# A transformer block on one core: another order of the linear steps, residual rows in a key buffer, and a planner that counts the port of VectorE and GpSimd both ways

## The chip, the core and the metric

The kernel runs on one core of a Trainium2 chip. The metric is device time in microseconds (us), from the first to the last instruction of one launch; of the kernel before there are three timed runs, and one further execution was recorded by the hardware profiler. In the profile the engines are called PE (TensorE matmuls), PEld (its weight loads), DVE (VectorE), ACT (ScalarE), POOL (GpSimd) and SP (SyncE, which issues the DMAs). "L205" is line 205 of the kernel before.

## What is computed

A conditioned (adaLN) transformer block on x of 8 sequences of 1024 tokens by 512 features, all in float32, with 16 heads of 32 features and a hidden layer of 2048:

```python
mod = silu(condition) @ Wada + bada
sh_a, sc_a, gt_a, sh_m, sc_m, gt_m = jnp.split(mod, 6, axis=1)
xm = layernorm(x, g1, be1) * (1.0 + sc_a[:, None, :]) + sh_a[:, None, :]
x = x + gt_a[:, None, :] * attention(xm, Wqkv, Wproj, bproj)     # causal, 16 heads
xm = layernorm(x, g2, be2) * (1.0 + sc_m[:, None, :]) + sh_m[:, None, :]
h = gelu(xm @ W1 + b1, approximate=False)
x = x + gt_m[:, None, :] * (h @ W2 + b2)
```

## The kernel before, in words

**Blocks.** A sequence is cut into two halves of 512 tokens. A half is a block; there are 16, numbered 0 to 15, and an odd one attends to its own keys and to those of the even one ahead of it. So even blocks carry little attention and odd ones much, and the work repeats from pair to pair.

**Two streams.** One stream is attention. For each block and each group of four heads it makes score tiles (`scores`, L1602 on PE), of which DVE masks the diagonal (L1616) and takes the maxima (L1619); the maxima are split into three bfloat16 parts (L1638 to L1641, on POOL or DVE), turned into a row by PE (L1657) and copied by ACT (L1663). Then come the weights: PE subtracts the maxima (L1683) and forms the transposed scores (L1695), ACT takes the exponential (L1708), POOL clears the upper triangle (L1713), PE multiplies with v (L1736), and POOL adds the weights up for the denominator (L1821), which PE sums at a group's end (L1757). Score tiles and weight tiles share one PSUM tile of four banks, named st or sc: the next user of it waits until DVE or ACT is through with the last.

The other stream is linear work: the projections k, q, v (`k`, `q`, `v`), the attention output with the gate and the residual (`proj`), the norm and modulation (`norm_a` and `at` for attention, `mt` for the hidden layer, with PE transposes at L769), the hidden layer up (`u`, four steps) and down (`d`, four parts). Nearly all of its matmuls come from one helper, L205. They follow Strassen's scheme with 7 products in place of 8, each of 256 columns; a full step of 7 products is 448 rows of the trace. The sums of that scheme are elementwise work: from PSUM by DVE (L197) or ACT (L192), and from SBUF to SBUF by a helper `either` that takes DVE (L162) or POOL (L165). The down part has two such subtractions on the hidden tiles hT, of 128 by 1024 elements each, that always go to DVE (L1211), and two that `either` places. Three PSUM banks serve the linear stream, the transposes, L1657 and L1757.

**The planner.** The order of all instructions is written by the kernel's own Python code. It keeps a clock for PE, DVE, ACT and POOL (`now`) and the time at which each buffer is written and left (`written`, `left`). Attention goes in its fixed order; between two of its units, `step_aside` puts in linear matmuls until the next unit is due by these clocks. `plan[w]` lists the linear steps of window w, that is, beside the attention of block w. `note` books an instruction; with `port=True` it is a DVE instruction that has to let a POOL instruction under way finish first. `either` takes DVE where it would end more than `margin` ns ahead of POOL. `sooner` chooses between DVE and ACT.

**Order of a window.** Window w finishes the down parts of block w-2 or w-1, projects v of block w, makes the attention output of block w-1, k of w+1, `mt` of w-1, q of w+1, and then the up steps of w-1. The residual rows of a block (`load_xr`, four DMAs of 256 KB by SP) lie in the single buffer of pool `xrp`; only block 14 used a key buffer. Keys have three buffers in turn.

**DMA.** Weights come through a ring of nine tiles of 256 KB (`fetch`), issued by SP in the order in which they are used, one tile to each of the 7 products.

Of the kernel before, what the change touches and what calls it, by code (L numbers as in the profile page):

```python
# [22 lines left out]
def kernel(  # L23
# [80 lines left out]
    def due(reads=(), writes=()):  # L104
# [4 lines left out]
            t = max(t, left.get(k, 0.0))  # L109
        return t  # L110

    def note(engine, ns, reads=(), writes=(), port=False):
        start = max(now[engine], due(reads, writes))
        if port:
            start = max([start] + [b for a, b in pool_spans if a <= start < b])
        end = start + ns
        now[engine] = end
        if engine == "POOL":
            pool_spans.append((start, end))
            del pool_spans[:-16]  # L120
# [28 lines left out]
        t = due(reads, writes)  # L149
        return "DVE" if max(now["DVE"], t) + dve <= max(now["ACT"], t) + act else "ACT"  # L150

    margin = [1500]

    def either(out, a, b, op, reads, writes):

# [82 lines left out]
        0: [("load_xa", 2), ("preps",), ("k", 1), ("norm_a", 2), ("gates", "a"), ("q", 1)]  # L238
        + [("mod", 4), ("at", 2), ("v", 1), ("mod", 3), ("gates", "m")],
    }  # L240
    late = []
    for w in range(1, NB):
        n = w - 1
        m = mlp_steps(n)
        even = blocks[n][1] == 0
        rows_a = [("rows", blocks[n][0], "a")] if even else []
        rows_m = [("rows", blocks[n][0], "m")] if even else []
        own = m[:1] + ([("load_xa", w + 2)] if w + 2 < NB else []) + m[1:3]
        own += [("norm_a", w + 2)] if w + 2 < NB else []
        if w == NB - 1:  # L250
            steps = late[:1] + [("load_xr", n)] + rows_a + [("proj", n), ("mt", n)] + late[1:]
            steps += [("v", w)] + rows_m + own + m[3:6]
            late = m[6:]
        else:

            steps = late + [("v", w), ("load_xr", n)] + rows_a + [("proj", n), ("k", w + 1)]
            if w == 1:
                steps = [("load_xr", n)] + rows_a + [("k", w + 1), ("proj", n)]
            steps += [("mt", n), ("q", w + 1)] + rows_m + own
            at = [("at", w + 2)] if w + 2 < NB else []  # L260
            if blocks[w][1] == 0:

                late = m[3:4] + at + m[4:]
            else:
                steps += m[3:4] + at + m[4:6]
                late = m[6:]
        plan[w] = steps
    n = NB - 1
    plan[NB] = [("load_xr", n), late[0], ("beside", ("proj", n)), late[1], ("mt", n)] + mlp_steps(n)

    plain_proj = (NB - 2, NB - 1)
    kept_sums = {}
# [538 lines left out]
        return bank  # L811

    qTs, kTs, vs = {}, {}, {}
    projected, valued = set(), set()
    xm_of, hTs, hidden = {}, {}, set()

    SUMS = (("S1", "A21", "A22", ALU.add), ("S2", "S1", "A11", ALU.subtract),
# [78 lines left out]
    def strassen(step, x, dest, target, row, done, put=None, after={}):  # L896
# [91 lines left out]
        tail_key[0] = key  # L988
        start(tail())

    def project_T(step, store, pool, tag, done):

        n = step[1]
        dst = pool.tile([P, NC, TB], F32, tag=tag, name=f"{tag}_{n}")
# [335 lines left out]
    def perform(step):  # L1330
        kind = step[0]
        if kind == "mod":
            yield from modulation(step[1])
        elif kind == "columns":
            parameter_columns()
        elif kind == "turn":
            yield from turn_first()
        elif kind == "gates":
            yield from gates(step[1])
        elif kind == "load_xa":  # L1340
            x_pre[step[1]] = load_x(step[1])
            written["x", f"a{step[1]}"] = now["PE"] + 6000
        elif kind == "load_xr":
            n = step[1]
            b, h = blocks[n]
            if n == NB - 2:
                xr = kvp.tile([P, NTT, D], F32, tag="kT", name=f"xr_{n}")
            else:
                xr = xrp.tile([P, NTT, D], F32, tag="xr", name=f"xr_{n}")
            residual[n] = xr  # L1350
            for t in range(NTT):
                r0 = h * TB + t * P
                nc.sync.dma_start(xr[:, t, :], x[b, r0 : r0 + P, :])
                landed = max(now["PE"], stored.get(n, 0.0)) + LANDING + 700 * t
                written["xr", n, t] = landed
        elif kind == "norm_a":
            key = f"a{step[1]}"
            normalize(x_pre.pop(step[1]), key, [("x", key)] * NTT)
        elif kind == "at":
            n = step[1]  # L1360
            guards = [("m used", n - 3)] if n > 2 else [("v done", 0)] if n == 2 else []
            start(modulated(f"a{n}", *columns_of["a"], blocks[n][0], guards))
        elif kind == "beside":
            start(perform(step[1]))
        elif kind == "sums":
            sum_weights(step[1:])
        elif kind == "mt":
            n = step[1]
            guards = [("v done", n + 1)]
            start(modulated(f"m{n}", *columns_of["m"], blocks[n][0], guards))  # L1370
        elif kind == "k":
            yield [("free for k", step[1])], []
            yield from project_T(step, kTs, kvp, "kT", lambda: None)
# [450 lines left out]
    def attend():  # L1824
        previous = None
        for n in range(NB):
# [19 lines left out]
            stream["rate"] = planned_time(n) / mine * (0.7 if n == 0 else 1.0)  # L1846
            written["free for k", n + 2 if n % 2 else n + 1] = 0.0
            written["free for k", n + 1] = 0.0
            for g, k, n_slots, upto in slots:
                if (n, g) == groups[-1]:  # L1850
                    margin[0] = -2000
# [66 lines left out]
    needs = sum(exp_need(parts) for n in range(NB) for g in range(NC) for parts in weight_units(n, g))  # L1918
    needs += sum(score_need(*unit) for unit in units)
    for n in range(NB):  # L1920
        written["attended", n] = NEVER
# [81 lines left out]
```

## Time and profile before

| quantity | value |
|---|---|
| median of 3 runs | 3485.39 us (3484.59 to 3486.25) |
| the profiled execution, time | 3487.44 us |
| the profiled execution, span of the core | 3485.7 us |
| PE busy | 3448.3 us, 99% |
| DVE busy | 1905.0 us, 55% |
| ACT busy | 1286.7 us, 37% |
| POOL busy | 2074.5 us, 60% |
| HBM over the span | 132 GB/s |

How to read it: the profiled execution lies within 0.1% of the median. PE has work nearly all of the time, so that the waits that count are short and many; they are found in the list of what PE waited for, and in the timeline around single waits. A matmul's row in the timeline gives the start of a run of like matmuls and the time until the last has drained; because matmuls are pipelined, the time from the start of one run to the start of the next is the better measure of what the first one takes.

### The profile page before, as it was taken

The page shows a single profiled execution, that of the slowest core. Times are in us where ns is not written, and L with a number is a line of the kernel's source. Part 1 is how long each engine was busy: PE and PEld are TensorE (multiplying, and loading weights), DVE is VectorE, ACT ScalarE, POOL GpSimd, SP SyncE. Part 2 cuts the span into 40 slices and gives each one's busy share as a digit, 9 for nine tenths or more (in the row PEclk, how much of TensorE's full clock was granted, in tenths as well). Part 3 has the DMA queues.
Part 4 walks back from the last instruction along what each step waited for, and adds up shares of the span by engine and source line. Part 5 has one row for each costly group of instructions (what it writes and reads, how often), then busy time and mean ns, then how long its engine had stood idle before and what let it go on. Part 6 is the DMA issues. An engine that isn't in the chain of part 4 may idle for free.

```text
span 3485.7 us, 122756 instructions
## 1 busy us (share of the span) xinstructions
PE 3448.3 (99%) x55618; PEld 1776.1 (51%) x55618; DVE 1905.0 (55%) x2136; ACT 1286.7 (37%) x1420; POOL 2074.5 (60%) x2209
## 2 busy tenths in 40 slices
PE   8999999999999999999999999999999999999999
PEld 5544455445554554545545455454554545545445
DVE  6765664554645556465564655645546455554463
ACT  2335243352433524235152352514524244241531
POOL 3676755675466664576645766557664576644640
PEclk9999999999999999999999999999999999999999
DMA  6843334335353353633536335363443534435334
GB/s 213 271 144 86 117 110 150 120 105 172 107 167 102 105 174 104 186 95 100 173 98 186 98 111 159 101 186 98 129 140 101 183 101 135 130 100 153 90 121 136
DMA packets 350523, 466.84 MB, mean 134 GB/s; under 512 B 27460, under 2 KB 212092, under 8 KB 350004
## 3 DMA queue, kind: packets, MB, share of 16 engines
q1 hardware_dynamic: 349808, 458.73, 43.8%
q8 instruction: 438, 7.18, 0.9%
q14 instruction: 81, 0.66, 0.1%
q10 hardware_dynamic: 196, 0.28, 0.0%
HBM read 416.90 MB, written 41.99 MB: 132 GB/s over the span
## 4 chain that ended last, share of the span: by engine, by line
PE 94%; DVE 3%; POOL 1%; ACT 1%; issue 0%; DMA 0%; SPq 0%; DVEq 0%; ACTq 0%; POOLq 0%
PE bank L205 65%; PE sc L1602 9%; PE po L1736 8%; PE st L1695 7%; PE st L1683 3%; DVE mx L1619 2%; PE bank L1757 2%; PE bank L769 1%; PE bank L1657 1%; POOL pT L1821 0%; DVE sc L1616 0%; POOL mcols L1640 0%; DVE pT L1818 0%; POOL mcols L1641 0%; DMA ada<-in_L_cond_Wada_dram 0%
## 5 line engine op out<-in xcount | busy, mean ns | idle before, releaser
L1821 POOL TENSOR_TENSOR pT<-pT,pT 128x256 f32<-128x256 f32 (+3 forms) x1254 | 1174.5, 972 | 210.3 <-ACT pT L1708 119.2
L1708 ACT ACTIVATE pT<-st 128x2048 f32<-128x2048 f32 x288 | 541.1, 1879 | 1001.1 <-PE st L1695 908.8
L205 PE MATMUL bank<-w,hT 128*32 128x256 f32 x14336 | 795.5, 379 | 0.0
L1619 DVE TENSOR_REDUCE mx<-sc 128x4 f32<-128x2048 f32 (+3 forms) x384 | 665.6, 1754 | 140.3 <-PE sc L1602 133.7
L205 PEld LDWEIGHTS bank<-w,hT 128*32 128x32 f32 x14336 | 448.8, 110 | 335.6 <-issue 29.2
L205 PE MATMUL bank<-xm_m,w 128*32 128x256 f32 x8192 | 498.8, 380 | 0.0
L205 PE MATMUL bank<-t_m,w 128*32 128x256 f32 x6144 | 384.2, 380 | 0.1
L205 PEld LDWEIGHTS bank<-xm_m,w 128*32 128x32 f32 x8192 | 253.6, 110 | 238.8 <-issue 76.0
L1713 POOL TENSOR_SCALAR_AFFINE_SELECT pT<-pT 128x512 f32<-128x512 f32 x256 | 164.8, 661 | 308.8 <-ACT pT L1708 306.9
L1602 PE MATMUL sc<-kT,qT 32*128 32x512 f32 (+3 forms) x3072 | 329.1, 520 | 2.9 <-DVE mx L1619 1.9
L1616 DVE TENSOR_TENSOR sc<-sc,mask 128x1024 f32<-128x1024 f32 (+1 forms) x160 | 162.9, 1018 | 276.2 <-PE sc L1602 217.6
L1736 PE MATMUL po<-pT,v 128*32 128x512 f32 (+3 forms) x3072 | 306.0, 493 | 0.0
L1695 PE MATMUL st<-qT,kT 32*128 32x512 f32 (+3 forms) x3072 | 299.8, 486 | 0.0
L205 PEld LDWEIGHTS bank<-t_m,w 128*32 128x32 f32 x6144 | 193.0, 110 | 180.8 <-issue 54.2
L205 PE MATMUL bank<-xm_a,w 128*32 128x256 f32 x3968 | 248.8, 381 | 1.3 <-ACT xm_a L784 1.1
L197 DVE TENSOR_TENSOR hT<-bank,u_u 128x512 f32<-128x512 f32 x192 | 129.1, 686 | 151.2 <-PE bank L205 149.0
L165 POOL TENSOR_TENSOR qT<-top,rec 128x512 f32<-128x512 f32 x60 | 77.1, 1285 | 219.8 <-ACT rec L1775 219.8
L1602 PEld LDWEIGHTS sc<-kT,qT 32*128 32x128 f32 x3072 | 129.4, 183 | 150.9 <-ACT pT L1708 61.8
L205 PE MATMUL bank<-w,qT 128*32 128x256 f32 (+1 forms) x2944 | 191.4, 399 | 1.3 <-DVE qT L1782 1.3
L1153 ACT ACTIVATE hT<-hT,cols 128x512 f32<-128x512 f32 x256 | 164.2, 711 | 55.0 <-DVE hT L197 54.4
L205 PE MATMUL bank<-t_a,w 128*32 128x256 f32 x2944 | 183.3, 380 | 0.0
L165 POOL TENSOR_TENSOR hT<-hT,hT 128x1024 f32<-128x1024 f32 x28 | 79.7, 2868 | 167.6 <-DVE hT L1211 167.6
(232 smaller groups left out, 3507.5 us busy)
## 6 DMA issues: line engine op xcount, KB each, us to landing
w<-in_L_cond_W_dram SPq DMA_DIRECT2D x384, 256.0 KB, 2.9
w<-kept_up_S SPq DMA_DIRECT2D x256, 256.0 KB, 2.6
w<-kept_down_S SPq DMA_DIRECT2D x256, 256.0 KB, 2.8
w<-kept_qkv_S SPq DMA_DIRECT2D x180, 256.0 KB, 2.7
w<-in_L_cond_Wqkv_dram SPq DMA_DIRECT2D x147, 256.0 KB, 3.0
hat<-in_x_dram SPq DMA_DIRECT2D x64, 256.0 KB, 4.7
xr<-in_x_dram SPq DMA_DIRECT2D x64, 256.0 KB, 4.6
out_dram<-xr SPq DMA_DIRECT2D x64, 256.0 KB, 2.6
```

What stands on the lines that cost most here:

```text
L165: nc.gpsimd.tensor_tensor(out, a, b, op)
L197: nc.vector.tensor_tensor(out, src, other, op)
L205: nc.tensor.matmul(ps[r, :], lhsT[:, r], rhs, start=start, stop=stop, skip_group_check=True)
L1153: nc.scalar.activation(hT[:, i, :], hT[:, i, :], AF.Gelu, bias=cols[:, O_B1 + f : O_B1 + f + 1])
L1602: nc.tensor.matmul(sc[:, j, c0 : c0 + w], qTs[n][r, gg, ts(qt, P)], keys_of(n, kh)[r, gg, :w], start=True, stop=True, skip_group_check=True,)
L1616: nc.vector.tensor_tensor(place, place, shape_of.to_broadcast(place.shape), ALU.add)
L1619: nc.vector.tensor_reduce(maxima[n, gg][:, kh, qt, :], sc[:, :, c0 : c0 + w], axis=AX.X, op=ALU.max)
L1695: nc.tensor.matmul(st[:, j, c0 : c0 + w], kT[r, gg, ts(k % NTT, P)], qT[r, gg, TB - w :], start=False, stop=True, skip_group_check=True,)
L1708: nc.scalar.activation(pT[:, :, :used], st[:, :, :used], AF.Exp, scale=scale)
L1713: nc.gpsimd.affine_select(diagonal, diagonal, pattern=[[0, HPG], [1, P]], compare_op=ALU.is_ge, fill=0.0, base=0, channel_multiplier=-1,)
L1736: nc.tensor.matmul(po[r, TB - w :], v[:, k % NTT, g * P + j * hd : g * P + (j + 1) * hd], pT[:, j, c0 : c0 + w], start=(k == 0), stop=last ...
L1821: nc.gpsimd.tensor_tensor(into, into, pT[:, j, c0 : c0 + w], ALU.add)
```

## The change

Four things are edited.

1. **The order of a window.** From window 3 on: the last up steps of block w-2 (they are now cut in two after the second step where block w is even), rows, residual load, v of w, the output of w-1, `mt` of w-1, then the four down parts of block w-2, then q and k of w+1, then the up steps of w-1. So the down parts are taken one window later than the hidden layer that they belong to, beside the norm of the next block.
2. **Residual rows.** Since a block's output is now made ahead of the down parts of the block before it, two blocks' residual rows are held at once: those of odd blocks go to an even key buffer that is free at that time, those of even blocks to the one buffer in `xrp`. The load waits in the plan for a new entry, "free for xr". Key buffers get fixed names. The first scores of a block wait in the plan for q and for k.
3. **The planner's port.** `note` now also holds a POOL instruction back while a DVE instruction that is booked with `port=True` runs (to 250 ns ahead of its end), and `give_way` moves POOL instructions that were already booked behind such a DVE instruction that starts before them.
4. `margin` goes from 1500 to 1000.

```diff
     shape = [None]
-    pool_spans = []
+    pool_spans, port_spans = [], []
+    FREE = 250
...
+    def give_way(start, end):
+
+        if not any(start <= a < end for a, *_ in pool_spans):
+            return
+        for i, (a, b, reads, writes) in enumerate(pool_spans):
+            if a < start:
+                continue
+            if a >= end:
+                break
+            later = end, end + b - a
+            pool_spans[i] = *later, reads, writes
+            for of, keys in ((left, reads), (written, writes)):
+                for k in keys:
+                    if of.get(k) == b + SYNC:
+                        of[k] = later[1] + SYNC
+            end = later[1]
+        now["POOL"] = max(now["POOL"], end)
+
     def note(engine, ns, reads=(), writes=(), port=False):
         start = max(now[engine], due(reads, writes))
         if port:
-            start = max([start] + [b for a, b in pool_spans if a <= start < b])
+            start = max([start] + [b for a, b, *_ in pool_spans if a <= start < b])
+            give_way(start, start + ns - FREE)
+        elif engine == "POOL":
+            start = max([start] + [b for a, b in port_spans if a <= start < b])
         end = start + ns
         now[engine] = end
-        if engine == "POOL":
-            pool_spans.append((start, end))
+        if port:
+            port_spans.append((start, end - FREE))
+            del port_spans[:-16]
+        elif engine == "POOL":
+            pool_spans.append((start, end, reads, writes))
             del pool_spans[:-16]
...
-    margin = [1500]
+    margin = [1000]
...
-    late = []
+    late, downs = [], []
     for w in range(1, NB):
...
-        own = m[:1] + ([("load_xa", w + 2)] if w + 2 < NB else []) + m[1:3]
-        own += [("norm_a", w + 2)] if w + 2 < NB else []
+        at = [("at", w + 2)] if w + 2 < NB else []
+        ups = m[:1] + ([("load_xa", w + 2)] if w + 2 < NB else []) + m[1:3]
+        ups += ([("norm_a", w + 2)] if w + 2 < NB else []) + m[3:4] + at
+        head = rows_a + [("load_xr", n)]
+        if w == 1:
+            steps = head + [("k", w + 1), ("proj", n), ("mt", n), ("q", w + 1)]
+        elif w == 2:
+            steps = downs[2:] + [("v", w)] + head + [("proj", n), ("mt", n), ("q", w + 1), ("k", w + 1)]
+        elif w < NB - 1:
+            steps = late + head + [("v", w), ("proj", n), ("mt", n)] + downs + [("q", w + 1), ("k", w + 1)]
+        else:
+            steps = late + head + [("v", w), ("proj", n), ("mt", n)] + downs
+        cut = m[2] if blocks[w][1] == 0 else None
+        i = ups.index(cut) if cut in ups else len(ups)
+        plan[w] = steps + rows_m + ups[:i]
+        late, downs = ups[i:], m[4:]
+        if w == 1:
+            plan[w] += downs[:2]
         if w == NB - 1:
...
-        else:
-
-            steps = late + [("v", w), ("load_xr", n)] + rows_a + [("proj", n), ("k", w + 1)]
...
-            steps += [("mt", n), ("q", w + 1)] + rows_m + own
...
+            plan[w] += late + downs[:2]
+            downs = downs[2:]
...
+    def key_tag(n):
+        return "odd_kT" if n % 2 else f"even_kT_{n // 2 % 2}"
...
-            if n == NB - 2:
-                xr = kvp.tile([P, NTT, D], F32, tag="kT", name=f"xr_{n}")
+            if n % 2:
+                yield [("free for xr", n)], []
+                spare = key_tag(min(n + 3, NB))
+                xr = kvp.tile([P, NTT, D], F32, tag=spare, name=f"xr_{n}", bufs=1)
             else:
                 xr = xrp.tile([P, NTT, D], F32, tag="xr", name=f"xr_{n}")
...
-                landed = max(now["PE"], stored.get(n, 0.0)) + LANDING + 700 * t
+                landed = max(now["PE"], stored.get(n - 1, 0.0)) + LANDING + 700 * t
...
-        until(lambda: units[unit_at[0]][0] in projected)
+        until(lambda: units[unit_at[0]][0] in projected & keyed)
```

The instructions themselves are the same in kind and number on PE; which of DVE, ACT and POOL takes an elementwise step is decided anew by the planner.

More of the change, by code (lines that the diff above doesn't have):

```diff
@@ L247 @@
         rows_m = [("rows", blocks[n][0], "m")] if even else []
-        own = m[:1] + ([("load_xa", w + 2)] if w + 2 < NB else []) + m[1:3]
-        own += [("norm_a", w + 2)] if w + 2 < NB else []
-        if w == NB - 1:
-            steps = late[:1] + [("load_xr", n)] + rows_a + [("proj", n), ("mt", n)] + late[1:]
-            steps += [("v", w)] + rows_m + own + m[3:6]
-            late = m[6:]
-        else:
-            steps = late + [("v", w), ("load_xr", n)] + rows_a + [("proj", n), ("k", w + 1)]
-            if w == 1:
-                steps = [("load_xr", n)] + rows_a + [("k", w + 1), ("proj", n)]
-            steps += [("mt", n), ("q", w + 1)] + rows_m + own
[L260 to L267, printed above, removed]
+        at = [("at", w + 2)] if w + 2 < NB else []
[16 more added lines that the diff above has]
+            plan[w] += downs[:2]
+        if w == NB - 1:
+            plan[w] += late + downs[:2]
+            downs = downs[2:]
     n = NB - 1
-    plan[NB] = [("load_xr", n), late[0], ("beside", ("proj", n)), late[1], ("mt", n)] + mlp_steps(n)
+    plan[NB] = [("load_xr", n), downs[0], ("beside", ("proj", n)), downs[1], ("mt", n)] + mlp_steps(n)
     plain_proj = (NB - 2, NB - 1)
@@ L813 @@
     qTs, kTs, vs = {}, {}, {}
-    projected, valued = set(), set()
+    projected, keyed, valued = set(), set(), set()
     xm_of, hTs, hidden = {}, {}, set()
@@ L1372, in perform @@
             yield [("free for k", step[1])], []
-            yield from project_T(step, kTs, kvp, "kT", lambda: None)
+            yield from project_T(step, kTs, kvp, "kT", lambda: keyed.add(step[1]))
         elif kind == "q":
@@ L1848, in attend @@
             written["free for k", n + 1] = 0.0
+            written["free for xr", n - 1] = 0.0
             for g, k, n_slots, upto in slots:
@@ L1920 @@
     for n in range(NB):
+        written["free for xr", n] = 0.0 if n == NB - 1 else NEVER
         written["attended", n] = NEVER
```

5 lines of the change are left out of this document (4 added, 1 removed).

## Prediction, made before the changed kernel ran

> **What bounds the kernel now.** I read the page first, then busy time by stretches, then what PE waited for, then the timeline around each kind of wait.
>
> ```profile
> PE 3448.3 (99%) x55618; PEld 1776.1 (51%) x55618; DVE 1905.0 (55%) x2136; ACT 1286.7 (37%) x1420; POOL 2074.5 (60%) x2209
> ...
> 989.00:1417.10 428.10, 426.74 (x6951) 219.43 (x6954) 230.02 (x258) 162.15 (x179) 263.45 (x279) 1.00 0.45 132
> ```
>
> PE is busy 99%. The second row is one pair of blocks, with the busy time of PE, PEld, DVE, ACT and POOL, at full granted clock (1.00): 428.10 us, PE busy for 426.74. The order of instructions shows as many PE instructions of each kind in the changed kernel. So its matmul time stays, and two things can change: what PE waits for, and what it pays where one form of matmul follows another. The waits, in the list for 420 to 3045 us (first three rows) and that for 80 to 420 us (last two):
>
> ```profile
> PE bank L1657 <- POOL mcols L1641: 4.4, 6, 0.7
> PE bank L769 <- ACT xm_m L784: 1.8, 6, 0.3
> PE sc L1602 <- DVE mx L1619: 1.4, 6, 0.5
> ...
> PE st L1683 <- DVE mx L1619: 2.4, 3, 1.5
> PE bank L1657 <- POOL mcols L1641: 1.3, 2, 0.6
> ```
>
> Six occurrences are one for each pair: a planned order that meets the same wait again and again. The list counts only idle time; what a wait costs is the lateness of a start against undisturbed matmuls, whose pace a long piece of the chain gives:
>
> ```profile
> 561.27 58.27 PE bank L205 x1080
> ```
>
> That is 54.0 ns for a row of 256 columns, 107.9 for one of 512.
>
> **The change, part by part.**
>
> *Waits of PE for the maxima rows (L1657).* In POOL's, DVE's and PE's timelines at the first of the six:
>
> ```profile
> 557.88 0.25 POOL L1638 CAST mcols<-mx 128x16 bf16<-128x16 f32 x1 [0.90 <-DVE mx L1633]
> 558.50 1.16 POOL L1640 CAST mcols<-rest 128x16 bf16<-128x16 f32 x1
> 559.74 1.07 POOL L1641 TENSOR_TENSOR mcols<-rest,mcols 128x16 bf16<-128x16 f32 x1
> 558.33 2.35 DVE L1211 TENSOR_TENSOR hT<-hT 128x1024 f32<-128x1024 f32 x2
> 559.05 1.07 PE L205 MATMUL bank<-w,hT 128*32 128x256 f32 x16
> 560.86 0.41 PE L1657 MATMUL bank<-ident_b,mcols 128*32 128x128 bf16 x16 [0.74 <-POOL mcols L1641]
> ```
>
> A split step of 0.25 us takes 1.16 and 1.07 while DVE's two subtractions run, and each ends as one of these ends: the two engines keep each other out. PE's 16 rows end at 559.05 + 16 x 0.054 = 559.91; L1657 starts at 560.86, 0.95 us late (0.92 without the few hundredths of a normal change). In the changed order the split of the odd block's second group is followed on DVE by steps that read PSUM (L197, v), not by L1211, and 9.4 us of PE work stand between the last scores and L1657 in place of 6.4. In even blocks the first two splits mostly go to DVE; no cover in the pairs is shorter than the shortest one of before (5.5 us), which caused no wait. Gain 6 x 0.92 = 5.5 us; bounds 0 and 5.5.
>
> *Waits between score tiles.* PE and DVE rows at one of them, with an undisturbed neighbour behind, and PE rows at the other kind:
>
> ```profile
> 1330.39 2.29 DVE L1619 TENSOR_REDUCE mx<-sc 128x4 f32<-128x2048 f32 x1
> 1330.62 1.93 PE L205 MATMUL bank<-xm_m,w 128*32 128x256 f32 x32
> 1332.73 0.71 PE L1602 MATMUL sc<-kT,qT 32*128 32x512 f32 x4 [0.18 <-DVE mx L1619]
> 1340.76 1.05 PE L205 MATMUL bank<-xm_m,w 128*32 128x256 f32 x16
> 1341.73 1.14 PE L1602 MATMUL sc<-kT,qT 32*128 32x512 f32 x8
> 1342.80 1.93 PE L205 MATMUL bank<-t_m,w 128*32 128x256 f32 x32
> ...
> 1370.32 0.64 PE L205 MATMUL bank<-xm_m,w 128*32 128x256 f32 x8
> 1370.78 1.91 PE L205 MATMUL bank<-t_m,w 128*32 128x256 f32 x32
> 1372.80 0.71 PE L1602 MATMUL sc<-kT,qT 32*128 32x512 f32 x4
> ```
>
> At 1340.76, 16 rows (0.86) and a change of form bring the scores at 1341.73: linear to scores costs 0.11. Scores to linear: 1342.80 - 1341.73 - 8 x 0.108 = 0.21. At 1330.62, 32 rows and the change end at 1332.46, the scores start 0.27 late; at 1370.32, 40 rows end at 1372.59, 0.21 late. In the second case the cover from the end of the scores is 0.21 + 40 x 0.054 + 0.11, about 2.5 us, against a reduction of 2.29 us and its latency of some 0.4. In the order, 14 scores have this short cover before the next; one has it in the changed kernel, the others at least 2.9 us. Gain 7 x 0.48 = 3.4. By the same count four other score tiles of the changed order come about 0.3 short: loss 1.1. Net gain 2.2; bounds 0 and 3.4.
>
> *Waits of the transposes.* PE rows and ACT's:
>
> ```profile
> 673.52 0.40 PE L205 MATMUL bank<-t_a,w 128*32 128x256 f32 x4
> 673.85 0.66 PE L769 MATMUL bank<-ident,xh_m 128*128 128x128 f32 x4
> 674.44 0.64 PE L205 MATMUL bank<-t_a,w 128*32 128x256 f32 x8
> 674.54 0.78 ACT L784 ACTIVATE xm_m<-bank,shiftm,gainm 128x512 f32<-128x512 f32 x1 [1.46 <-PE bank L769]
> 675.38 0.33 PE L769 MATMUL bank<-ident,xh_m 128*128 128x128 f32 x1 [0.30 <-ACT xm_m L784]
> ```
>
> Into a transposed bank that ACT empties until 675.32, PE comes back after 8 rows: it could start at 674.44 + 0.43 + 0.12 = 674.99 (0.12 from the first two rows) and is 0.39 late. Beside q and k, Strassen's scheme holds two banks; in the changed order `mt` runs beside the down parts, which hold one, and the transposes go in pairs into the other two. Gain 6 x 0.39 = 2.3; bounds 0 and 2.3.
>
> *The first pair (80 to 420 us).*
>
> ```profile
> 350.02 6.08 POOL L165 TENSOR_TENSOR hT<-hT,hT 128x1024 f32<-128x1024 f32 x2 [3.99 <-DVE hT L1211]
> 353.80 2.85 DVE L162 TENSOR_TENSOR qT<-top,rec 128x512 f32<-128x512 f32 x1
> 360.23 0.39 PE L1683 MATMUL st<-mrow,minus_ones 32*128 32x512 bf16 x4 [1.45 <-DVE mx L1619]
> ```
>
> A DVE product of 512 elements takes 2.85 us beside POOL's two long subtractions, so the maxima behind it are late and PE waits 1.45. In the changed kernel these subtractions are DVE's. That and the waits for L1657 there (1.3) may go: 2.8. But in block 0 one score tile of the fourth group gets 1.8 us of cover in place of a sufficient one, against a mask (0.70, by its row below), a reduction and latency of 0.7 + 2.3 + 0.4 = 3.4: loss 1.5. Net gain 1.3; bounds -3 and 4.
>
> *Changes of form.* Before there are 1101 between the forms of scores and of linear work and 131 from or to transposes; after, 1133 and 97. The first split into 17 more at 0.21 and 15 more at 0.11: 5.2 us. The second, 34 fewer at 0.12: -4.1. Loss 1.1; bounds 0 and 3.
>
> *Work that moves between engines.* The groups by line:
>
> ```profile
> L165 POOL TENSOR_TENSOR hT<-hT,hT 128x1024 f32<-128x1024 f32 x28 | 79.7, 2868 | 167.6 <-DVE hT L1211 167.6
> L165 POOL TENSOR_TENSOR hT<-hT 128x1024 f32<-128x1024 f32 x19 | 57.5, 3038 | 0.0
> L162 DVE TENSOR_TENSOR hT<-hT 128x1024 f32<-128x1024 f32 x13 | 19.4, 1508 | 0.0
> L1211 DVE TENSOR_TENSOR hT<-hT,hT 128x1024 f32<-128x1024 f32 x32 | 37.6, 1216 | 0.0
> L1821 POOL TENSOR_TENSOR pT<-pT,pT 128x512 f32<-128x512 f32 x504 | 633.2, 1290 | 121.8 <-ACT pT L1708 119.2
> L1713 POOL TENSOR_SCALAR_AFFINE_SELECT pT<-pT 128x512 f32<-128x512 f32 x256 | 164.8, 661 | 308.8 <-ACT pT L1708 306.9
> L1616 DVE TENSOR_TENSOR sc<-sc,mask 128x512 f32<-128x512 f32 x64 | 44.7, 699 | 134.4 <-PE sc L1602 107.3 <-issue 27.1
> L1616 DVE TENSOR_TENSOR sc<-sc,mask 128x1024 f32<-128x1024 f32 x96 | 118.2, 1231 | 141.8 <-PE sc L1602 110.3 <-ACT top L1770 12.2 <-ACT xh_m L653 11.5
> L1619 DVE TENSOR_REDUCE mx<-sc 128x4 f32<-128x1536 f32 x64 | 112.5, 1757 | 2.2
> ```
>
> POOL loses 28 + 18 of these: some 135 us of its 2074.5. DVE gains 46 at 1.22 to 1.51 us, 56 to 69 us on 1905.0. Both keep room, but DVE works in order, and it is tight at one place in each odd block: in the third group (six blocks, 3 to 13) a score tile's mask (1.23) and reductions (1.76 and a third of that) stand behind v3 (L197, as a mask of 512), two L1211 and two moved subtractions: 1.23 + 2.4 + 0.7 + 4 x 1.22 = 9.2 us of DVE work, with 8.6 of PE's from one tile's scores to the next. Counted on, DVE ends about 0.3 us ahead of PE's next weights if nothing holds it; with one hold by POOL's triangle step (0.66) it is 0.4 late. I take 0.2 x 6 = 1.2; what a worse case costs is a rival below.
>
> At this place a rule of the Trainium skill speaks against the change (SBUF — State Buffer, "SBUF: two separate sides"): a VectorE step with two inputs in SBUF and a GpSimd step that reads SBUF exclude each other for a whole instruction, and the one that starts first wins. The stretched 0.25 us steps and the 2.85 us product agree with it. By it, each moved subtraction also shuts out POOL's sums; that would change the result only where a sum is waited for.
>
> *At no cost.* The residual loads are 4 DMAs a block as before. SP stands at them until the last weights of a block have read the key buffer, with weight loads queued behind; nine tiles of 64 rows at 0.054 are 31 us of PE work, and that cover is longer than the tail of a block. Without it, each late tile would stop PE for its landing. The extra wait for k costs nothing while linear work is left to put in. I take 0 for the stretch after 3045 us, where the last steps are unchanged; bounds -3 and 3.
>
> **The sum.** 5.5 + 2.2 + 2.3 + 1.3 - 1.1 - 1.2 = 9.0 us off the profiled 3487.44 (span 3485.7), or 3478.4. The median lies 2.05 below that execution: 3485.39 - 9.0 = 3476.4.
>
> **The rivals.**
> - *The gain is given back in small new waits.* For: all scores are planned to within some 0.1 us of DVE's end, and DVE gets 56 to 69 us more. Against: fewer scores fall short by count. If half of the 10.0 us of the pairs returns, 3481.4.
> - *DVE is held by POOL's sums at the tight place; slower.* If the four subtractions there each let one sum of 1.29 us go first, DVE is 5.2 - 0.3 = 4.9 late, in six blocks 29 us: 3485.39 - 10.2 + 29 = 3504; with three holds, 3497. It decides from 17 us on, 2.9 us a block. For: POOL's sums are 633 us. Against: L1211's mean of 1.22 us over 32 shows them seldom held, and by the order POOL has just ended one set of sums there.
> - *All new tightness proves harmless.* All bounds on the good side, 5.5 + 3.4 + 2.3 + 4: 15.2 off, and 3 at the end: 3467.
> - *The planner changes nothing that PE feels,* the waits only move: 3485.
>
> **How the numbers follow.** The forecast has 0.50, the good side 0.12, the small new waits 0.19, no effect 0.06, the port 0.13. A measurement tells 0.2% (7 us) from no change: faster is below 3478.4, slower above 3492.4. The forecast, uncertain by some 4 us, lies below 3478.4 in nearly nine of ten: 0.45 with 0.12 is 0.57 faster; 0.05 + 0.19 + 0.06 is 0.30 the same; 0.13 slower. The range for 8 in 10 is 3466 to 3490; the forecast's own is 3470 to 3483.
>
> **What would show it.** Right: a pair of blocks near 426.5 us; no waits for L1641 and few for L1619 from 420 us on; POOL's hT groups nearly gone; L1640 and L1641 near 0.25 to 0.35. Wrong: a wait of L1683 for L1619 in every odd block, with L162 hT far over 1.22 us; waits for weight DMAs; or PE rows with more idle time after 3045 us.

## The result, and the profile after

| quantity | before | after |
|---|---|---|
| median | 3484.75 us (3483.65 to 3486.25, 9 runs) | 3496.5 us (3491.06 to 3500.8, 9 runs) |
| ratio to before, 95% interval | | 1.0032 (1.0022 to 1.0042) |
| the profiled execution | 3487.44 us | 3495.71 us |

The changed kernel is slower by 0.32%, where 0.2% can be told from no change; the forecast was 3476.4 us, and the time lies above the whole range. Its runs also differ by 10 us among themselves, those of before by under 3.

The head of the page after, and then busy time from 420 to 3045 us in the kernel before (first of the two rows) and after (second), columns as in the prediction:

```profile
span 3494.0 us, 122624 instructions
...
PE 3450.0 (99%) x55618; PEld 1792.7 (51%) x55618; DVE 2022.6 (58%) x2234; ACT 1289.5 (37%) x1438; POOL 1963.2 (56%) x2083
```

```profile
420.00:3045.00 2625.00, 2616.49 (x42600) 1346.80 (x42592) 1417.64 (x1590) 991.34 (x1090) 1621.29 (x1733) 1.00 0.44 131
```

```profile
420.00:3045.00 2625.00, 2604.52 (x42332) 1356.46 (x42324) 1522.56 (x1673) 990.90 (x1105) 1524.97 (x1610) 1.00 0.44 130
```

The loss is in the pairs of blocks: in the same 2625 us PE is idle 12.0 us longer (2616.49 - 2604.52). What it waits for there, in the list of waits of PE after, from 420 to 3045 us:

```profile
PE bank L230 <- ACT rec L1801: 11.1, 9, 2.7
PE bank L230 <- ACT xm_m L810: 2.4, 6, 0.4
PE sc L1636 <- ACT pT L1742: 1.8, 1, 1.8
PE bank L1691 <- POOL mcols L1675: 1.6, 1, 1.6
PE bank L795 <- ACT xm_m L810: 1.0, 1, 1.0
PE st L1717 <- DVE mx L1653: 0.8, 5, 0.2
...
PE sc L1636 <- DVE mx L1653: 0.6, 2, 0.3
```

Lines moved by some 25 to 35: L205 is L230 now, L1619 L1653, L1641 L1675, L1657 L1691, L1683 L1717, L1708 L1742, L784 L810. The six waits for POOL's split (4.4 us) are gone, and one of 1.6 us is new. Nearly all else that is new has ACT behind the arrow, that is, as its releaser: an engine that is busy 37% and whose new order the prediction did not cost. L1801 is the logarithm of a group's denominators: PE sums them into one of the three linear banks (L1791), and ACT's logarithm frees that bank.

**The place in odd blocks.** PE's, ACT's and SP's rows in the timeline after, in block 7 (start, duration, engine, line):

```profile
1435.50 0.38 SPq L751 DMA_DIRECT2D xm_a<-turned_a  x1
...
1439.94 1.04 PE L1791 MATMUL bank<-pT,ones 128*32 128x512 f32 x8
...
1441.98 0.64 PE L230 MATMUL bank<-w,qT 128*32 128x256 f32 x8
1442.60 2.22 ACT L810 ACTIVATE xm_a<-xm_a,shifta,gaina 128x512 f32<-128x512 f32 x3 [3.60 <-DMA w<-kept_down_S]
...
1444.73 0.57 ACT L1801 ACTIVATE rec<-bank 128x512 f32<-128x512 f32 x1
...
1445.36 4.49 PE L230 MATMUL bank<-w,hT 128*32 128x256 f32 x48 [2.73 <-ACT rec L1801]
```

PE's sums are in their bank by 1441, but ACT does its work in order, and ahead of the logarithm stands the modulation of the next block's rows (L810, input xm_a). Those rows are turned by way of DRAM: four writes (L745) and one load (L751). The load, issued at 1435.50, lets ACT go on at 1442.60; the name behind the arrow is another transfer that landed then, but L810 reads only the turned rows. ACT stands 3.60 us, takes 2.22 for the modulation, and then frees the bank. PE is idle for 2.73. The same in the list of ACT's waits from 420 to 3045 us, first before, then after:

```profile
ACT xm_a L784 <- DMA xm_a<-turned_a: 128.9, 10, 16.8
```

```profile
ACT xm_a L810 <- DMA xm_a<-turned_a: 14.4, 7, 5.9
```

The list puts some of these waits under other names, the 3.60 us of block 7 among them. Counted by the steps themselves, ACT stood at these rows for 157.8 us in twelve places before, and for 22.8 in eleven after. In the kernel before nothing of PE was behind it: copies of v came next, and ACT stood another 14.8 to 23.1 us at each of those. The new order makes v earlier, and the logarithm takes the place behind the rows.

**The clock.** Busy time after, in three stretches that follow on this wait (the granted clock is the third number from the end of a row):

```profile
1442.00:1445.40 3.40, 0.67 (x16) 0.18 (x15) 1.78 (x3) 2.80 (x5) 0.00 (x0) 1.00 0.42 114
1446.20:1449.60 3.40, 3.40 (x40) 1.78 (x36) 3.40 (x5) 0.11 (x1) 2.44 (x2) 0.55 0.09 8
1449.70:1453.00 3.30, 3.30 (x60) 1.71 (x52) 3.30 (x3) 0.00 (x0) 3.17 (x2) 1.00 0.35 84
```

After the idle time the clock is halved for about 3.4 us: 40 rows in place of 60. That is another 1.7 us, which no list of waits shows, since PE counts as busy. It comes a second time behind a wait of 2.20 us near 2735 us, and nowhere between 420 and 3045 us in the kernel before. How long ACT stands differs from pair to pair, and with it both prices; that this also makes the spread of 10 us is argued here, and tested below.

**The place in even blocks.** PE's and ACT's rows after, in block 8:

```profile
1615.93 1.04 PE L1791 MATMUL bank<-pT,ones 128*32 128x512 f32 x8
1616.31 1.28 ACT L1185 ACT_TABLE_LOAD   x1
...
1617.60 2.56 ACT L1185 ACTIVATE hT<-hT,cols 128x512 f32<-128x512 f32 x4
1617.98 3.23 PE L230 MATMUL bank<-xm_m,w 128*32 128x256 f32 x56
...
1620.18 1.28 ACT L170 ACT_TABLE_LOAD   x1
1621.47 0.60 ACT L1801 ACTIVATE rec<-bank 128x512 f32<-128x512 f32 x1
...
1622.12 1.94 PE L230 MATMUL bank<-t_m,w 128*32 128x256 f32 x32 [0.91 <-ACT rec L1801]
```

Here four GELUs, with a table load on each side, stand ahead of the logarithm: 5.1 us. PE's 56 rows end at 1617.98 + 56 x 0.054 = 1621.00, so the next start is 1.12 late; five such places make 5.6 us.

### The profile page after: what moved, and what is told of

Read it like the earlier page. It is cut to its first block, busy times and chain, and to the rows that moved or that the text cites. A ratio compares the mean times of both kernels' runs of the same rounds, so it can differ in the third digit from the quotient of the medians.

```text
span 3494.0 us, 122624 instructions
## 1 busy us (share of the span) xinstructions
PE 3450.0 (99%) x55618; PEld 1792.7 (51%) x55618; DVE 2022.6 (58%) x2234; ACT 1289.5 (37%) x1438; POOL 1963.2 (56%) x2083
## 4 chain that ended last, share of the span: by engine, by line
PE 93%; ACT 2%; DVE 2%; DMA 2%; issue 0%; SPq 0%; POOL 0%; ACTq 0%; DVEq 0%; POOLq 0%
PE bank L230 65%; PE sc L1636 8%; PE po L1770 7%; PE st L1729 7%; PE st L1717 3%; PE bank L1791 1%; DVE mx L1653 1%; PE bank L795 1%; DMA xm_a<-turned_a 1%; ACT pT L1742 1%; DMA turned_a<-xm_a 1%; PE bank L1691 0%; ACT xm_a L810 0%; ACT hT L1185 0%; DVE sc L1650 0%
## 5 line engine op out<-in xcount | busy, mean ns | idle before, releaser
L1855 POOL TENSOR_TENSOR pT<-pT,pT 128x256 f32<-128x256 f32 (+3 forms) x1254 | 1230.4, 1016 | 194.7 <-ACT pT L1742 123.5
L1742 ACT ACTIVATE pT<-st 128x2048 f32<-128x2048 f32 x288 | 540.9, 1878 | 1025.5 <-PE st L1729 907.9
L230 PE MATMUL bank<-w,hT 128*32 128x256 f32 x14336 | 821.5, 381 | 9.0 <-ACT rec L1801 6.6
L1653 DVE TENSOR_REDUCE mx<-sc 128x4 f32<-128x2048 f32 (+3 forms) x384 | 665.7, 1754 | 210.9 <-PE sc L1636 204.7
L230 PEld LDWEIGHTS bank<-w,hT 128*32 128x32 f32 x14336 | 454.4, 110 | 374.0 <-issue 82.0
L230 PE MATMUL bank<-xm_m,w 128*32 128x256 f32 x8192 | 499.9, 380 | 0.1
L1747 POOL TENSOR_SCALAR_AFFINE_SELECT pT<-pT 128x512 f32<-128x512 f32 x256 | 177.8, 712 | 445.2 <-ACT pT L1742 443.5
L230 PE MATMUL bank<-t_m,w 128*32 128x256 f32 x6144 | 384.2, 380 | 4.7 <-ACT rec L1801 4.6
L230 PEld LDWEIGHTS bank<-xm_m,w 128*32 128x32 f32 x8192 | 256.0, 110 | 223.1 <-issue 60.9
L230 PEld LDWEIGHTS bank<-t_m,w 128*32 128x32 f32 x6144 | 190.7, 110 | 181.7 <-issue 54.5
L230 PE MATMUL bank<-xm_a,w 128*32 128x256 f32 x3968 | 239.8, 381 | 2.0 <-ACT xm_a L810 1.1
L230 PE MATMUL bank<-w,qT 128*32 128x256 f32 (+1 forms) x2944 | 192.9, 399 | 0.0
L230 PE MATMUL bank<-t_a,w 128*32 128x256 f32 x2944 | 181.2, 380 | 0.0
L230 PEld LDWEIGHTS bank<-xm_a,w 128*32 128x32 f32 x3968 | 127.4, 110 | 95.6 <-issue 12.6
```

Of the source, the lines that this page charges most:

```text
L230: nc.tensor.matmul(ps[r, :], lhsT[:, r], rhs, start=start, stop=stop, skip_group_check=True)
L1653: nc.vector.tensor_reduce(maxima[n, gg][:, kh, qt, :], sc[:, :, c0 : c0 + w], axis=AX.X, op=ALU.max)
L1742: nc.scalar.activation(pT[:, :, :used], st[:, :, :used], AF.Exp, scale=scale)
L1747: nc.gpsimd.affine_select(diagonal, diagonal, pattern=[[0, HPG], [1, P]], compare_op=ALU.is_ge, fill=0.0, base=0, channel_multiplier=-1,)
L1855: nc.gpsimd.tensor_tensor(into, into, pT[:, j, c0 : c0 + w], ALU.add)
```

## The experiments

The theory that was tested: ACT's queue, with the turned rows and the GELUs ahead of the logarithm, costs what the change was to gain and more. The main rival: DVE's added load and the port that it shares with POOL. All times are medians; the kernel before ran beside each, at 3484.1 to 3485.4 us.

**e1_order_alone.** The changed kernel with `note` and `margin` of before.

```diff
-            give_way(start, start + ns - FREE)
-        elif engine == "POOL":
-            start = max([start] + [b for a, b in port_spans if a <= start < b])
...
-    margin = [1000]
+    margin = [1500]
```

> The new order of work with the residual rows in a key buffer, but the planner's accounting of before (DVE waits for POOL only, margin 1500). Theory, ACT's queue: the waits of PE that the changed kernel has come from the order of the work (the turned rows' modulation, L810, stands ahead of the logarithm, L1801, which frees the bank of the product with d; four GELUs stand ahead of it in even blocks), so they stay: 3492 to 3500 us, at least 10 of the 13 waits of a bank for L1801 still there. Rival, the port: the cost comes from the accounting that moves hT subtractions to DVE; without it the time is at or below the kernel before's, 3477 to 3486 us, with POOL's busy time back near 2070 us.

3509.88 us, ratio 1.0068 (1.0056 to 1.0081): 13.4 above the changed kernel. Its waits of PE from 420 us on (lines are 25 lower there: L1666 is L1691, L1692 L1717, L1717 L1742, L1776 L1801):

```profile
PE bank L1666 <- ACT pT L1717: 8.3, 4, 2.1
PE st L1692 <- DVE mx L1628: 6.2, 10, 1.1
PE bank L205 <- ACT rec L1776: 6.0, 8, 0.9
```

Neither theory gave so much. The logarithm is waited for in 8 places, not 10, and waits at the maxima come on top. The name in the first row misleads: at one of its places the exponential (L1717) and POOL's last split step both end at 1498.81, and what L1666 reads is the split:

```profile
1498.54 0.27 POOL L1650 TENSOR_TENSOR mcols<-rest,mcols 128x16 bf16<-128x16 f32 x1
...
1498.85 0.23 PEld L1666 LDWEIGHTS <-mcols 128*32 128x32 bf16 x16 [2.26 <-POOL mcols L1650]
```

This is a wait for POOL's split, of the kind that the change was to remove, here 2.1 us long and in five places (four in the first row). So the new accounting does not cause the loss: within the new order it saves 13 us. By the rival the time should have fallen.

**e2_port_alone.** The plan and buffers of before, with the new accounting and margin.

```diff
+            give_way(start, start + ns - FREE)
+        elif engine == "POOL":
+            start = max([start] + [b for a, b in port_spans if a <= start < b])
...
-    margin = [1500]
+    margin = [1000]
```

> The order and the buffers of before with the new accounting alone (ports both ways, margin 1000). Theory, ACT's queue: copies of v stand behind the turned rows as before and nothing of PE waits for them; DVE's load rises by some 50 us without harm: 3479 to 3486 us, with the six waits of the maxima rows for POOL's split (0.92 us each) fewer or gone, and no stretch of halved clock after 420 us. Rival, the port: DVE is late at the score tiles and the time is that of the changed kernel or above, 3493 to 3500 us.

3519.02 us, ratio 1.0096 (1.0081 to 1.0112): 34 us above the kernel before. One row of its waits carries most of it (L1708 is L1683 of before, L1644 L1619):

```profile
PE st L1708 <- DVE mx L1644: 20.9, 24, 1.1
```

DVE's maxima are late four times in a pair. The theory's number was wrong, and for this order the rival holds. But the same accounting that costs 34 us here saves 13 in the new order, so it has no price of its own.

**e9_margin_alone.** The kernel before with the margin alone.

```diff
-    margin = [1500]
+    margin = [1000]
```

> The kernel before with one number of the accounting changed, the margin at 1000 ns in place of 1500. Theory: few hidden sums change engine, so the time stays within 3 us of the kernel before, 3482 to 3489 us, and the 34 us that the new accounting alone cost (e2_port_alone) come from DVE and POOL counted as holding each other, which moves scores in the order. Rival: the order of before is so finely set that any change of the planner's counts costs tens of us: 3500 us or more.

3502.58 us, ratio 1.005 (1.0036 to 1.0064): half of those 34 us from one number. The rival's time is right, and the theory's first step was wrong: many hidden sums change engine. Of the 64 that `either` places, POOL had 47 before and has 13 here, as many as in e2_port_alone. So half of that kernel's loss comes with these moves, and the other half with the counting of the port. Whether DVE's load or the shifted order is what costs is not shown. Its waits are small and come six times each, once a pair; two of its rows:

```profile
PE sc L1602 <- ACT pT L1708: 4.6, 6, 0.8
PE bank L1657 <- POOL mcols L1641: 4.5, 6, 0.7
```

**e3_rows_later.** The changed kernel, with the planner told that the turned rows land 10 us after the issue of their load.

```diff
-            written["spread", key] = queue_free[0] + 5000
+            written["spread", key] = queue_free[0] + 10000
```

> The changed kernel with one number changed: the planner takes the turned rows as landed 10 us after the queue has issued their load, not 5, so ACT's order becomes logarithm, copy, exponential and then the modulations that wait for the rows. Theory, ACT's queue: the six waits of PE for a bank that L1801 frees in odd blocks (13.1 us of lateness in all in the changed kernel's profile) and the two stretches of halved clock behind them vanish: 10 to 13 us less than the changed kernel, 3483 to 3487 us, and runs of it that agree within 3 us rather than 10. The five waits behind the GELUs (1.12 us each) stay. Rival, the DMA itself: the rows are late for whatever comes next, the up projection then waits, and the time stays at 3493 us or more. Rival, the port: no change, 3494 to 3499 us.

3483.03 us (3481.86 to 3485.22, 11 runs), ratio 0.9994 (0.9985 to 1.0003): 13.5 below the changed kernel, and the spread is down to 3.4 us. The same place in its timeline:

```profile
1435.89 0.38 SPq L751 DMA_DIRECT2D xm_a<-turned_a  x1
...
1441.06 0.60 ACT L1801 ACTIVATE rec<-bank 128x512 f32<-128x512 f32 x1 [2.13 <-PE bank L1791]
...
1442.56 2.93 ACT L810 ACTIVATE xm_a<-xm_a,shifta,gaina 128x512 f32<-128x512 f32 x4
...
1444.10 0.61 PE L230 MATMUL bank<-w,hT 128*32 128x256 f32 x8
```

The load is issued within 0.4 us of the same time, and ACT does the logarithm and two more steps before it turns to the rows; the modulation then waits for nothing, and PE goes on at 1444.10. Of the waits of PE for L1801 only the five of even blocks are left:

```profile
PE bank L230 <- ACT rec L1801: 4.5, 5, 0.9
```

In the whole list from 420 to 3045 us PE's waits fall from 20.0 to 10.1 us, and no stretch there has its clock halved. This is the theory as it was put, in time, places and spread.

**e6_no_puts.** The order of the changed kernel (ACT's differs by a few steps between 670 and 700 us and nowhere else), but the four writes of turned rows are left out and the load reads x as it lies, so the blocks from the fifth on are computed from other data.

```diff
-                for a in range(P // SQ):
-                    transfers.append((ready, lambda a=a: put(a)))
...
-            nc.sync.dma_start(xm, there.rearrange("(c p) n -> p c n", p=P))
+            b, h = blocks[int(key[1:])]
+            nc.sync.dma_start(xm, x[b, h * TB : h * TB + TB, :].rearrange("(c p) n -> p c n", p=P))
```

> The changed kernel, whose order of instructions stays, without the four writes of a block's normalised rows to DRAM: the load that read them back turned reads the input rows as they lie instead, so blocks from the fifth on are computed from other data. That load needs to wait for no write and can start at once. Theory, ACT's queue with the DMA's round trip ahead of it: the load is done before ACT comes to the modulation, the six waits in odd blocks fall from 13.1 us of lateness to under 3, no halved clock: 3482 to 3488 us. Rival, ACT is late of its own work (its queue is full at that place whether or not the rows are there): the waits stay near 1 us or more in each odd block and the time at 3490 us or above. Rival, the port: 3494 to 3499 us.

3482.26 us (3481.24 to 3484.31), ratio 0.9991 (0.9983 to 1.0): 14.2 below the changed kernel with ACT's order kept. Of the waits for the logarithm, again, only the five of even blocks are left (4.5 us). So it is the lateness of the rows, not ACT's own work, that ACT stands for in odd blocks; either remedy removes the same 13 to 14 us.

**e4_ln_first.** The changed kernel, with a slot's GELUs given out behind the closing of the slot before, in all blocks.

```diff
                 pT, slot = weights_T(n, g, parts)
-                run_excursions(1)
                 pace(exp_need(parts))
                 maxima_rows()
                 if previous is not None:
                     close(*previous)
+                run_excursions(1)
```

> The changed kernel with the GELUs and the rows' modulation of a slot (run_excursions) given out behind the closing of the slot before, which has the logarithm. Theory, ACT's queue: the waits behind the GELUs (five places, 1.12 us of lateness each, in even blocks) go; in odd blocks the turned rows are taken up earlier, while their transfer is still on its way, so ACT stands at them before the exponential and the logarithm, and the waits there stay or grow: 3488 to 3510 us. Rival: any logarithm given out sooner helps, 3480 to 3487 us.

3525.77 us, ratio 1.0118 (1.0104 to 1.0132): worse than either theory said. PE's and ACT's rows in an odd block:

```profile
1405.43 0.60 ACT L1801 ACTIVATE rec<-bank 128x512 f32<-128x512 f32 x1 [3.44 <-PE bank L1791]
...
1407.05 1.28 ACT L1185 ACT_TABLE_LOAD   x1
...
1410.93 1.28 ACT L170 ACT_TABLE_LOAD   x1
1412.22 1.88 ACT L1742 ACTIVATE pT<-st 128x2048 f32<-128x2048 f32 x1
...
1414.15 0.62 PE L1717 MATMUL st<-mrow,minus_ones 32*128 32x512 bf16 x4 [3.66 <-ACT pT L1742]
```

The logarithm is early, but the GELUs now stand ahead of the next exponential (L1742), and PE waits 3.66 us for it, with a halved clock behind. The expected place (the turned rows) was not the one. It is the same queue all the same: what moves behind an ACT step delays the step after it.

**e7_both_late.** e3_rows_later, with the GELUs behind the closing in even blocks alone.

```diff
-                run_excursions(1)
+                if h:
+                    run_excursions(1)
...
+                if h == 0:
+                    run_excursions(1)
```

> Two edits in the changed kernel: the turned rows counted as landed after 10 us (as in e3_rows_later), and in even blocks alone the GELUs given out behind the logarithm. Theory, ACT's queue: on top of what e3_rows_later gained, the five waits of 1.12 us behind the GELUs go: 5 to 6 us below e3_rows_later's 3483.0, so 3477 to 3478.5 us, at or near the 3476.4 us that was forecast for the change. Rival: the logarithm is not what these five places wait for, or the wait comes back at another place: 3481.5 to 3485 us.

3480.51 us, ratio 0.9988 (0.9979 to 0.9997): half of what was expected. The waits for L1801 are gone from its list, but others grew:

```profile
PE bank L230 <- ACT xm_m L810: 3.6, 5, 0.7
PE st L1717 <- DVE mx L1653: 2.1, 6, 1.2
```

**e10_ln_later_blocks.** The same, with the GELUs moved only from block 4 on.

```diff
-                if h:
+                if h or n < 4:
...
-                if h == 0:
+                if h == 0 and n >= 4:
```

> e7_both_late with the logarithm ahead of the GELUs only from block 4 on, so that blocks 0 to 3 keep the changed kernel's order of slots. Theory: e7_both_late gained 2.6 us of lateness over e3_rows_later from block 3 on and gave 1 to 2 us of it back in blocks 1 to 3 (lateness at the start of block 2: 10.0 us against 8.6 and 6.6); without that, 1 to 3 us below its 3480.5: 3477.5 to 3479.5 us. Rival: the early blocks' lateness is a matter of when the first transfers land and differs from run to run: 3480 to 3482 us.

3477.08 us (3476.22 to 3478.42), ratio 0.9979 (0.997 to 0.9988): faster than both kernels, by 7.0 and 19.4 us. The theory's number came out, slightly better. What e7_both_late lost in its first blocks is known in part: its profile has a stretch of halved clock at 219 us, worth 1.7 us, and this kernel's has none. The wait that remains in its pairs:

```profile
PE bank L230 <- ACT xm_m L810: 4.4, 6, 0.7
```

**e11_dve_evac.** e10_ln_later_blocks, with every second transposed bank emptied by DVE.

```diff
+            if turned is None and not rows_turned and key[0] == "m":
+                on_dve = c % 2
```

> e10_ln_later_blocks with every second evacuation of a transposed bank (L784 in the kernel before, L810 in the changed one) put on DVE instead of left to the planner, which gives nearly all of them to ACT. Theory of the transposes: PE's remaining waits for ACT's xm_m (in e7_both_late 3.6 us of idle time in five places, 1.1 us of lateness each) come from two evacuations in a row on ACT behind an exponential of 1.9 us; alternated, they fall to under 0.3 us each: 4 to 6 us below e10_ln_later_blocks, at 3472 to 3476 us. Rival: DVE, which already has the maxima and the hidden sums, is late at the scores instead: no gain or up to 20 us more, 3478 to 3500 us.

3487.4 us, ratio 1.0009 (1.0 to 1.0018): the expectation failed, the rival holds. Waits of PE from 420 us on (lines are 2 higher there):

```profile
PE bank L230 <- ACT xm_m L812: 6.3, 6, 1.1
PE st L1719 <- DVE mx L1655: 3.3, 6, 2.4
```

The wait that it was to remove is longer, and DVE's maxima are late too. Whether another sharing would help stays open.

**e8_pool_ht.** e7_both_late, with the hidden sums back on POOL.

```diff
-    margin = [1000]
+    margin = [6000]
```

> e7_both_late with the planner's margin for DVE at 6000 ns in place of 1000, so that 47 of the hidden sums (hT) are POOL's, as in the kernel before; the order of the work stays. Theory: with the waits for ACT gone, the hidden sums on DVE are what took away POOL's split waits and DVE's late product; back on POOL they cost 3 to 12 us: 3481 to 3490 us, with waits for mcols (L1675) back. Rival, the port: DVE's added load is the cost, and without it the time falls by 2 us or more, to 3475 us or less.

3519.84 us, ratio 1.01 (1.0086 to 1.0114): 39 us more than e7_both_late, and no sign of the rival. But most of the loss lies in the first blocks and is not the port's alone. In the profiled execution (3524.6 us, the slowest of four) PE is idle for 24.6 of the 390 us from 30 to 420 us, against 7.4 in e7_both_late. One wait for weights is a good part of it, and one of 4.5 us for other weights comes on top:

```profile
PE bank L230 <- DMA w<-kept_qkv_S: 6.5, 1, 6.5
```

Some 34 us up to 430 us run at half the clock besides. From pair to pair only some 2.9 us are added: the same wait for L810 comes every 430.4 us here and every 427.5 in e7_both_late. There the port does show, in POOL's and DVE's rows behind a set of transposes:

```profile
1521.59 4.93 POOL L1855 TENSOR_TENSOR pT<-pT,pT 128x512 f32<-128x512 f32 x4
...
1522.92 1.22 DVE L1672 CAST mcols<-mx 128x16 bf16<-128x16 f32 x1
...
1524.17 1.17 DVE L1673 TENSOR_TENSOR rest<-mx,mcols 128x16 f32<-128x16 f32 x1
```

Steps that take about 0.2 us when POOL is not in the way (0.25 in the rows of before) take 1.2 each, one for each of POOL's sums. The port is shared as the prediction read it. With this planner the sums are cheaper on DVE; how much of the 39 us is the port's stays open.

## Why the prediction was wrong

**The step that failed** is *At no cost*. It asked of the moved steps what they do to SP's queue, to the key buffer and to the wait for k, and it had the terms of DVE, POOL and PE elsewhere. ACT had a term at the transposes alone; what the new order does to ACT's queue, and through it to the three banks, was put at nothing without a reason. Moving v ahead takes away what stood behind the turned rows on ACT. Their row in the waits of before, 128.9 us, was a sign of it: so long a wait cost nothing only because nothing that PE needs soon stood behind it. The new order of ACT shows L1801 straight behind L810 in five of the six odd blocks from 3 to 13 and, in block 3, behind L810 and an exponential. The Trainium skill says in "TensorE: Matmul & The Clock Gate", section "Architectural detail: the array is 16× 32×32, not 1× 128×128", that ACT and DVE are strictly first in, first out. The trace agrees: the sums are in their bank by 1441, and the logarithm starts at 1444.73, behind 3.60 us of standing and 2.22 of modulation, with PE idle for 2.73.

**The sum closes with it.** From the forecast to the result there are 3496.5 - 3476.4 = 20.1 us. e3_rows_later takes away 13.5 (the rows), e10_ln_later_blocks another 5.9 (the logarithm behind the GELUs, 5.6 by the trace); 0.7 are left. So the two places on ACT, 13.5 and 5.9 us, are what the step left out. That the rest agrees so well is partly luck, since its terms were off in both directions:
- *Waits for POOL's split* (gain 5.5): right for the six of before; one place in block 4 is new, with 1.6 us of idle time.
- *Score tiles* (gain 2.2): too high. The waits of scores for the maxima, 1.4 us in six places, became 0.8 in five at L1717 and 0.6 in two at scores, so by idle time nothing was gained.
- *Transposes* (gain 2.3): wrong. Before, 1.8 us in six places; after, 2.4 and 1.0. They go in pairs into two banks, but ACT empties both, one behind the other, and the product behind them waits instead.
- *First pair* (gain 1.3): right. PE is busy 336.00 us of the stretch from 80 to 420 us, before 334.40. The wait of 1.45 us is gone, and one of 1.86 at 115.50 us is new.
- *Changes of form* (loss 1.1): the counts came out, 32 more and 34 fewer in the two traces. What they cost was not measured.
- *The tight place on DVE* (loss 1.2): it did not come. In block 7 four subtractions in a row begin at 1483.92, the reductions behind them end at 1492.50, and PE's next weights start at 1493.50 without idle time. The five waits of L1717 (0.8 us) lie elsewhere, in block 7 at 1403.62 behind a step of the norm and two sums from PSUM. That is partly luck, since DVE's added load was sized too low: 117.6 us (2022.6 - 1905.0) in place of 56 to 69. The moved subtractions alone take longer than the 1.22 to 1.51 us that were taken for them, in their larger group 1.67:

```profile
L187 DVE TENSOR_TENSOR hT<-hT,hT 128x1024 f32<-128x1024 f32 x32 | 52.1, 1668 | 0.0
```

- *Residual loads and SP's queue* (none): right, no tile of weights is waited for from 420 us on.
- *The end* (0): 1.6 us gained, within the bound. PE's only wait there is 1.7 us, before 3.3 in five.

**The rivals.** The one on the slower side (DVE held by POOL's sums, 3497 to 3504 us) named the sign and nearly the time, but not the cause: with the rows out of the way the time is 3483.0 with the sums still on DVE, no wait stands behind the four subtractions of the tight place, and taking the sums off DVE did not help (e8_pool_ht). "Given back in small new waits" (3481.4) is what the change is without the turned rows: 3483.0 and 3482.3. Of what would have shown the forecast wrong, waits for weights did not come, and L1683's wait came in five odd blocks with 0.16 us each, far too little. A pair, which was to take near 426.5 us, took 428.7 (from the wait at 1622.12 us to its like at 2050.85). The list asked for the engines that had been costed.

## What to carry to other kernels

Before costing a reorder, list for each in-order engine where it stands waiting for something off the critical path, and look up in the new order what comes next behind that place: a long wait that costs nothing is one whose follower nobody needs. Count every shared resource with a release, the PSUM banks here, together with the engine that releases it, however idle that engine is on average. In a schedule that runs against planned times, a late arrival that is assumed too early puts its reader ahead of urgent work; assuming it late cost nothing here and was worth 13.5 us.

## What the runs showed of the hardware

A pause of PE of little over 2 us can halve its clock for the next 3.4 us. In e1_order_alone a wait of 2.1 us comes at the same place of five pairs. Busy time of that kernel behind the first of them, in the second, and behind the second (the granted clock is the third number from the end):

```profile
1066.80:1069.80 3.00, 3.00 (x56) 1.16 (x43) 2.97 (x2) 0.58 (x1) 3.00 (x2) 1.00 0.02 5
...
1496.80:1498.90 2.10, 0.04 (x4) 0.05 (x8) 1.96 (x4) 1.88 (x1) 1.88 (x5) 1.00 0.39 113
1499.30:1502.30 3.00, 3.00 (x28) 1.01 (x23) 2.96 (x2) 0.59 (x1) 3.00 (x2) 0.50 0.00 0
```

The same pause leaves the clock whole the first time and halves it the second, 56 rows against 28 in 3 us; of the five, three were followed by a halved stretch. Shorter pauses did it too: in e8_pool_ht one of 1.82 us at 1095.12, the first of five alike, and in e7_both_late four of 0.16 to 0.58 us in a row, with PE busy for 2.51 of the 4.00 us from 214.8 to 218.8. The Trainium skill ("TensorE: Matmul & The Clock Gate", sections "What's actually happening" and "Why this matters for your kernels") has a free-running window of about 3.4 us, an idle one of which drops the clock, and advises against gaps over about 3 us. The length and the play of chance agree; the bound does not, since 2.1 us were enough.

And a planner's constant can be worth more than the edit that it goes with: 500 ns of margin, which moved 34 sums to another engine, cost the kernel before 17.6 us.
